# A graph-attention layer on one core: seven parts in stacked tables, and the edge term over 64 rows and 128 columns

## The chip, the cores and the metric

The kernel runs on one core of a Trainium2 chip. The metric is device time in microseconds of the whole launch, as the median of several runs. A profiled execution gives one trace beside it.

## What is computed

A graph layer over N = 12500 nodes of 128 features and E = 412500 edges with 64 features each; `dst` is sorted. It ends in two layer normalisations. The reference, cut to what matters:

```python
h = x @ Wn + bn;  q = x @ Wq + bq;  k = x @ Wk + bk;  v = x @ Wv + bv
eh = edge_attr_64 @ We + be
attn_in = concatenate([q[src], k[dst], eh], axis=-1)
hmid = leaky_relu(attn_in @ A1 + b1, 0.2)
scores = leaky_relu(hmid @ A2 + b2, 0.2)          # 8 heads
w = softmax(scores.mean(axis=-1), axis=0)         # over all edges
out = segment_sum(w[:, None] * v[dst], src, N)
y = layernorm(h + out) * gamma + beta
return layernorm(x + y)
```

The first layer `A1` is folded into the weights of q, k and the edge term, so that the hidden value of an edge is a sum of a q row (by `src`), a k row (by `dst`) and 64 edge features times a 64 x 128 matrix.

## The kernel before

Edges come sorted by `dst`, but sums are wanted by `src`. So the kernel has two halves that run interleaved.

*Making.* The edges stand in 403 groups of 1024, eight tiles of 128. For each group `make` builds one record per edge: 128 numbers of k plus edge term, 128 of v, and the source's place in its block. The k and v rows are picked by a one-hot matmul (`ohd` with `kvs`, bfloat16), and the edge term is added into the same PSUM tile `pkv` by a float32 matmul of `eat` with `WeS`. A `pkv` tile holds four edge tiles, so a group has two of them (two half-groups). In `eat` the features of tiles 0 to 3 of a group lie on partitions 0 to 63 and those of tiles 4 to 7 on partitions 64 to 127; `WeS` is a matrix of 128 rows and two times 128 columns whose off-diagonal quarters are zero, so that one matmul of 128 rows and 256 columns gives the edge term of one tile from each half. ScalarE copies `pkv` into a record tile `rec` (six buffers), and POOL scatters it to DRAM with one indirect DMA per tile, eight a group, into a table `rtab` in which every block of 128 nodes has its own stretch of `cap` rows. VectorE counts edges per block to find the rows (`few`, `ats`, `pos`, `idx`).

*Consumption.* The groups are divided into parts by `PARTS`; a part writes one of two tables in turn. Within a part there are stops: by a stop, so many tiles of every block are full with certainty, and these can be read back while the rest is written. The tiles of all 98 blocks between two stops are a round. A round is read in units of three blocks: one load `rt` of 3 x t tiles (t tiles per block, 4 or 5), then q rows by a one-hot matmul, the hidden layer (`ph`, `hm`), scores (`psc`), a running maximum, weights `w`, and the weighted sum of v rows into `psm`, which is added to the sum of the round before (`old`, kept in DRAM as `atab`). Scheduled steps of a unit are spread by `lags`; the order in which the two halves are written down is set in `sorted_path`: step lists of the rounds are laid between the six pieces of each group, from `begun[r]` on, at a pace that `PACE` sets. What remains after the last group follows alone, then `closing` normalises.

With `PARTS = (74, 140, 165), (225, 278, 307), (367, 403)` a part has 15, 13 and 9 tiles per block, 37 in all, in eight rounds of 5, 5, 5, 4, 4, 5, 4 and 5. A table holds 15 tiles per block (`cap`). Tiles that a part may leave short are filled with zeros in the first two parts (`fill`, `zeros`), and masked in the last round of a part (`masks`). Before the first round's stop, tables of q, k, v and h rows are made in pieces between the groups (`tables`, `later`), and ready by nine tenths of that stop.

All engines run their queues in order. SP issues nearly all plain DMAs in one queue: edge features and `kvs` rows four groups ahead of their use, loads and stores of units, zero fills. POOL issues the scatters; a scatter waits for its `rec` and `idx` and for the scatter eight before it.

The lines that the change and the prediction touch: L931 one-hot matmuls and L936 edge term; L946 and L947 the copies into `rec`; L958 the scatter; L1144 the load of a unit; L1243, L1247 hidden layer; L1258 scores; L1284 sum over heads; L1305 to L1323 maximum and weights; L1375 the weighted sum.

Of the kernel before, what the change touches and what calls it, by code (L numbers as in the profile page):

```python
# [10 lines left out]
FP = mybir.dt.float32  # L11
# [24 lines left out]
PARTS = (74, 140, 165), (225, 278, 307), (367, 403)  # L36
NP = len(PARTS)
NR = sum(map(len, PARTS))
# [11 lines left out]
class Plan:  # L50
# [4 lines left out]
    def __init__(self, n, e, nb, groups):  # L55
# [15 lines left out]
        most = max(self.tiles)  # L71
# [24 lines left out]

    def bounds(self):

        first = np.arange(self.nb + 1) * self.cap
        out = [first] * NP  # L100
        for p, g, t0, t in self.rounds:
            full = np.array([(t0 + t) * P] * self.nb + [0])
# [5 lines left out]
        return np.array(out, np.float32)  # L108

# [362 lines left out]
def sorted_path(  # L472
# [112 lines left out]
    WeS = const.tile([P, 2, D], FP)  # L585
# [26 lines left out]
    with tc.tile_pool(name="prep", bufs=1) as prep, tc.tile_pool(  # L612
# [164 lines left out]
    maskp = pool("mask", 1)  # L777
# [12 lines left out]
    masks, placed, lims = {}, {}, {}  # L790
    last_rounds = [r for r, q in enumerate(plan.rounds) if q[1] == plan.parts[q[0]][1]]
# [13 lines left out]
    def make(p):  # L805
# [118 lines left out]
        def rows(g, j):  # L924

            (eat, kvs), ohd = data[g], ohds[g]
            pk = pkvp.tile([P, 2, 2, 2 * D], FP, name="pkv")
            for i in range(2):
                for h in range(2):
                    t = h * (GT // 2) + j + i  # L930
                    nc.tensor.matmul(  # L931
                        pk[:, i, h, :], ohd[t], kvs,
                        start=(h == 0), stop=False,
                    )
            for i in range(2):
                nc.tensor.matmul(  # L936
                    pk[:, i, :, :D], eat[:, (j + i) * P : (j + i + 1) * P], WeS,
                    start=False, stop=True,
                )
            return pk  # L940

        def evacuate(g, j, pk):
# [7 lines left out]
                .rearrange("p (h t o) -> p t h o", h=2, o=1)[:, j : j + 2, :, :]  # L950
# [3 lines left out]
            for h in range(2):  # L954
                for i in range(2):
# [16 lines left out]
                    tc.add_to_no_dep_group(f"rows{p}.{at}", one_tile)  # L972
                    if p == 0 and g < plan.gate:
# [132 lines left out]
    def sums_of(bp):  # L1106
# [805 lines left out]
```

## Time and profile before

| | |
|---|---|
| median of 3 runs | 4827.88 us (4826.07 to 4830.85) |
| the profiled execution | 4829.19 us, of which the span of instructions 4827.2 us |
| mean granted TensorE clock | 0.916 |
| busy: PE, DVE, ACT, POOL | 3991.6, 4064.7, 3144.8, 3304.4 us |
| DMA moved | 1484.41 MB, mean 308 GB/s |
| first scatter begins, last ends | 59.3 us, 4283.7 us |

The page lists for each engine busy time and share, then the span in 40 slices with a digit for tenths of busy time. Rows of groups read: line, engine, operation, output and inputs with shapes, count, then busy time and mean duration of one in ns, then idle time ahead of them and what ended it. A wait row reads: who waited, for whom, microseconds in all, times, longest. Rows in order of time read: start, length, engine, line, operation, count. PE rows are matmul passes, PEld rows weight loads; matmuls are pipelined, so the start of one to the start of the next says more than the length of one.

### The profile page before, as it was taken

To read this page: it belongs to the slowest core of one execution; us is meant where nothing else is said; L and a number is where in the kernel's file an instruction comes from. 1 tells how busy PE (TensorE), PEld (TensorE's weight loads), DVE (VectorE), ACT (ScalarE), POOL (GpSimd) and SP (SyncE) were. 2 spreads that over 40 slices of the span, in tenths; PEclk is the share of its full clock that TensorE was granted. 3 is DMA by queue.
4 is the path that set the end of the run, shared out by engine and by line. 5 is a ranking of instruction groups with operands and counts; after the bars stand their busy time and mean duration, and the time that the engine had idled before them with its cause. 6 is when DMAs were issued, how large, how long until landed. Compare 5 with 4: busy or idle time off the path is not lost. (4 is left out here: it accounts for less than half of the span.)

```text
span 4827.2 us, 84360 instructions
## 1 busy us (share of the span) xinstructions
PE 3991.6 (83%) x26680; PEld 3111.2 (64%) x26680; DVE 4064.7 (84%) x8217; ACT 3144.8 (65%) x8198; POOL 3304.4 (68%) x3279
## 2 busy tenths in 40 slices
PE   3556655577788999999999999998998899998997
PEld 2334433466666777777777666666777777666777
DVE  8878886688878999999998888888999988877767
ACT  2432222366666778787787777777777777777886
POOL 3777777777777777777777777777777777741103
PEclk7877785899888999999999999999999999999999
DMA  6888887888988999999999999999999999989964
GB/s 196 282 279 288 286 298 243 294 300 298 296 299 299 358 336 334 333 348 337 323 335 324 329 331 329 332 336 325 342 332 326 333 316 334 320 294 327 318 215 176
DMA packets 599153, 1484.41 MB, mean 308 GB/s; under 512 B 100352, under 2 KB 299923, under 8 KB 596902
## 3 DMA queue, kind: packets, MB, share of 16 engines
q1 hardware_dynamic: 436350, 1049.04, 65.4%
q0 software_dynamic: 154752, 429.39, 23.3%
q8 instruction: 212, 3.47, 0.3%
q14 instruction: 247, 2.02, 0.1%
q10 hardware_dynamic: 7592, 0.48, 0.1%
HBM read 906.61 MB, written 611.06 MB: 314 GB/s over the span
## 5 line engine op out<-in xcount | busy, mean ns | idle before, releaser
L958 POOL DMA_INDIRECT rtab<-rec,idx x3224 | 3219.2, 999 | 1061.2 <-issue 777.2
L946 ACT ACTIVATE rec<-pkv 128x1024 f32<-128x1024 f32 x806 | 822.2, 1020 | 1120.4 <-DMA rtab<-rec,idx 572.8
L1346 ACT ACTIVATE ohw<-ohs,w 128x128 f32<-128x128 bf16 x3626 | 1189.1, 399 | 75.7 <-DVE ohs L1332 27.2
L1375 PE MATMUL psm<-rt,ohw 128*128 128x128 f32 x7252 | 1023.1, 285 | 1.1 <-ACT ohw L1346 1.0
L1375 PEld LDWEIGHTS psm<-rt,ohw 128*128 128x128 f32 x7252 | 943.9, 197 | 76.1 <-ACT hm L1243 7.7
L936 PE MATMUL pkv<-WeS,eat 128*128 128x256 f32 x3224 | 946.4, 421 | 0.0
L1247 DVE TENSOR_TENSOR hm<-ph,hm 128x512 f32<-128x512 f32 (+1 forms) x949 | 627.4, 661 | 300.9 <-ACT hm L1243 299.0
L931 PE MATMUL pkv<-kvs,ohd 128*128 128x256 bf16 x3224 | 539.1, 295 | 373.6 <-ACT rec L946 370.2
L931 PEld LDWEIGHTS <-ohd 128*128 128x128 bf16 x3224 | 320.9, 105 | 645.9 <-issue 531.8
L936 PEld LDWEIGHTS pkv<-WeS,eat 128*128 128x128 f32 x3224 | 620.2, 214 | 75.0
L1224 PE MATMUL ph<-ident,rt 128*128 128x128 f32 x3626 | 587.2, 284 | 64.5 <-DVE hm L1247 63.6
L1210 DVE TENSOR_SCALAR ohT<-rowB,iotaP,power 128x512 bf16<-128x512 uint8 (+2 forms) x1274 | 598.9, 492 | 34.8 <-DMA rowB<-row 34.6
L1243 ACT ACTIVATE hm<-ph 128x512 f32<-128x512 f32 (+1 forms) x949 | 537.5, 566 | 84.1 <-PE ph L1233 29.2
L1224 PEld LDWEIGHTS ph<-ident,rt 128*128 128x128 f32 x3626 | 418.3, 146 | 269.7 <-issue 145.5
L1233 PE MATMUL ph<-ohT,qs 128*128 128x512 bf16 (+2 forms) x2548 | 559.7, 323 | 16.1 <-DVE ohT L1210 11.3
L872 DVE TENSOR_SCALAR ohd<-dstb,node 128x1152 bf16<-128x1152 uint8 x404 | 565.0, 1399 | 4.5 <-PE pkv L931 4.5
L900 DVE TENSOR_TENSOR ats<-pc,oh 128x792 f32<-128x792 f32 x403 | 392.2, 973 | 61.7 <-PE pc L880 56.6
L1332 DVE TENSOR_TENSOR ohs<-iotaE,sl 128x512 bf16<-128x512 bf16 (+1 forms) x949 | 404.6, 426 | 5.0 <-ACT ohw L1346 4.8
L862 DVE TENSOR_REDUCE few<-oh 128x99 bf16<-128x792 bf16 x403 | 395.1, 980 | 13.9
L911 DVE TENSOR_REDUCE pos<-ats 128x8 f32<-128x792 f32 x403 | 390.7, 970 | 2.5
L1258 PE MATMUL psc<-hm,A2s 128*32 128x512 f32 (+1 forms) x1898 | 345.9, 607 | 31.9 <-DVE hm L1247 23.7
L1284 PEld LDWEIGHTS psm<-headsum,z 96*128 96x128 f32 (+2 forms) x2112 | 259.7, 193 | 32.8 <-issue 8.3
(190 smaller groups left out, 3790.5 us busy)
## 6 DMA issues: line engine op xcount, KB each, us to landing
rt<-rtab SPq DMA_DIRECT2D x160, 1950.0 KB
rt<-rtab SPq DMA_DIRECT2D x96, 1560.0 KB
eat<-in_ea SPq DMA_DIRECT2D x201, 512.0 KB
rtab<-rec,idx POOLq DMA_INDIRECT x3224
dstb<-dtab SPq DMA_DIRECT2D x201, 256.0 KB
qs<-qtab SPq DMA_DIRECT2D x256, 192.0 KB
atab<-old SPq DMA_DIRECT2D x256, 192.0 KB
old<-atab SPq DMA_DIRECT2D x224, 192.0 KB
```

The source lines that it names most:

```text
L872: nc.vector.tensor_scalar(to, row[:, cols], node, None, op0=ALU.is_equal)
L931: nc.tensor.matmul(pk[:, i, h, :], ohd[t], kvs, start=(h == 0), stop=False,)
L936: nc.tensor.matmul(pk[:, i, :, :D], eat[:, (j + i) * P : (j + i + 1) * P], WeS, start=False, stop=True,)
L946: nc.scalar.activation(rec[:, :, :, : 2 * D], pk, AF.Copy)
L958: one_tile = nc.gpsimd.indirect_dma_start(out=rtab[p % TABS][:, :], out_offset=bass.IndirectOffsetOnAxis(ap=idxs[g][:, t : t + 1], axis=0) ...
L1210: nc.vector.tensor_scalar(st["oh"][k][:, (a - t0) * P : (b - t0) * P], st["rowB"][:, a * P : b * P], iotaP, power[:, bs[u] : bs[u] + 1], o ...
L1224: nc.tensor.matmul(ph[:, j * P : (j + 1) * P], st["rt"][:, t0 + j, :D], ident, is_transpose=True, start=(j == 0), stop=False,)
L1233: nc.tensor.matmul(ph[:, cols], st["qs"][:, j0 // t, s, :], oh[:, cols], start=False, stop=(s == 1 and j1 == t0 + n),)
L1243: nc.scalar.activation(hm, state[i]["ph", k][:, : n * P], AF.Copy, scale=SLOPE)
L1247: nc.vector.tensor_tensor(hm, ph[:, : n * P], hm, op=ALU.max)
L1346: nc.scalar.activation(ohw[:, j, :], ohs[:, :, j], AF.Copy, scale=st["w"][:, t0 + j : t0 + j + 1])
L1375: nc.tensor.matmul(st["psS"][:, (1 + u) * P : (2 + u) * P], ohw[:, j, :], st["rt"][:, t0 + j, D : 2 * D], start=(k == 0), stop=(k == t - 1),)
```

## The change

It does five things. The parts become seven, ending at groups 96, 192, 243, 283, 323, 363 and 403, with stops at 60 and 156 inside the first two. That makes 9, 9, 5, 4, 4, 4 and 4 tiles per block, 39 in all, in nine rounds of 4, 5, 4, 5, 5, 4, 4, 4 and 4. The two tables shrink from 15 to 9 tiles per block, and parts may share a table at different heights: `TABLE` says which table, `ABOVE` from which tile on; parts whose tiles don't meet are told apart, so that neither waits for the other. The load of a part's last round waits for the last eight scatters of that part. The edge term is cut in two: each half of the rows of `eat` and `WeS` (64 partitions) gives its own tile by a matmul of 64 rows and 128 columns; `pkv` and `rec` are laid out half first, so that the two halves write different halves of the `pkv` tile. A second buffer for `mask`.

```diff
-PARTS = (74, 140, 165), (225, 278, 307), (367, 403)
+PARTS = (60, 96), (156, 192), (243,), (283,), (323,), (363,), (403,)
 NP = len(PARTS)
+TABLE = (0, 1, 0, 0, 1, 1, 0)
+ABOVE = (0, 0, 0, 5, 0, 4, 0)
...
-        most = max(self.tiles)
+        most = max(t + above for t, above in zip(self.tiles, ABOVE))
...
+        while any(abs(self.gate - g) < 6 for _, g, *_ in self.rounds):
+            self.gate -= 1
...
+    def apart(self, p, q):
+        a, b = ABOVE[p], ABOVE[q]
+        return p != q and TABLE[p] == TABLE[q] and (
+            a >= b + self.tiles[q] or b >= a + self.tiles[p]
+        )
...
-    WeS = const.tile([P, 2, D], FP)
+    WeS = const.tile([P, D], FP)
...
-        nc.vector.memset(WeS, 0.0)
-        for h in range(2):
-            half = slice(h * DE, (h + 1) * DE)
-            nc.vector.tensor_copy(WeS[half, h, :], We_[half, :])
+        nc.vector.tensor_copy(WeS, We_)
...
-    maskp = pool("mask", 1)
+    maskp = pool("mask", 2)
...
+            for h in range(2):
+                for i in range(2):
+                    nc.tensor.matmul(
+                        pk[:, h, i, :], ohd[h * (GT // 2) + j + i], kvs,
+                        start=(i == 0), stop=False,
+                    )
             for i in range(2):
                 for h in range(2):
-                    t = h * (GT // 2) + j + i
+                    half = slice(h * DE, (h + 1) * DE)
                     nc.tensor.matmul(
-                        pk[:, i, h, :], ohd[t], kvs,
-                        start=(h == 0), stop=False,
+                        pk[:, h, i, :D], eat[half, (j + i) * P : (j + i + 1) * P], WeS[half, :],
+                        start=False, stop=(i == 1),
                     )
-            for i in range(2):
-                nc.tensor.matmul(
-                    pk[:, i, :, :D], eat[:, (j + i) * P : (j + i + 1) * P], WeS,
-                    start=False, stop=True,
-                )
...
-                        out=rtab[p % TABS][:, :],
+                        out=rtab[TABLE[p]][:, :],
...
-                        in_=rec[:, i, h, :], in_offset=None,
+                        in_=rec[:, h, i, :], in_offset=None,
...
+                    for q in range(NP):
+                        for k in range(len(PARTS[q]) if plan.apart(p, q) else 0):
+                            for name in "rows", "loads":
+                                tc.declare_no_dep(
+                                    one_tile, group=f"{name}{q}.{k}", reason="other tiles"
+                                )
...
-            o = lags(p, nk)
+            o = lags(p, max(nk, 3))
...
+            t0 += ABOVE[p]
...
-                in_=rtab[p % TABS][bs[0] * cap : (bs[0] + m) * cap, :]
+                in_=rtab[TABLE[p]][bs[0] * cap : (bs[0] + m) * cap, :]
...
+            if r == of_part[-1]:
+                for one in tail_of[p][-GT:]:
+                    tc.add_manual_dep(
+                        rows_in, one.name, mybir.DependencyInfo(
+                            mybir.DependencyClass.Sync, mybir.DependencyReason.DATA
+                        ), reason="records of the part",
+                    )
```

TensorE, one half-group in the middle of the program, before. `ohd` and `kvs` are the one-hot and the k and v rows, `eat` the edge features, `few` the counts of a block; the last number is the size of the output.

```order
L931 MATMUL pkv<-kvs,ohd 128x256
L936 MATMUL pkv<-WeS,eat 128x2x128 x2
L880 LDWEIGHTS rest
L880 MATMUL pc<-few,rest 128x99
L1224 MATMUL ph<-ident,rt 128x128 x3
```

And a half-group there now:

```order
L944 MATMUL pkv<-kvs,ohd 128x256
L951 MATMUL pkv<-WeS,eat 128x128 x4
L894 LDWEIGHTS rest
L894 MATMUL pc<-few,rest 128x99
L1257 MATMUL ph<-ident,rt 128x128 x4
```

Two matmuls of 256 columns have become four of 128 between the same neighbours.

SP's queue at the first load of consumption, before. `eat` and `kvs` are the loads of the making, `dstb` the ids of destinations, `rt` a unit's load from table `rtab0`, and `rtab1<-zeros` fills the second table.

```order
L818 DMA eat_6065<-in_ea 128x1024
L822 TENSOR_LOAD start_224
L827 ISA
L827 DMA kvs_6070<-kvtab_65 128x256
L1144 DMA rt_6086<-rtab0_76 128x3x1300
```

And now:

```order
L832 DMA eat_5522<-in_ea 128x1024
L836 TENSOR_LOAD start_223
L841 ISA
L841 DMA kvs_5527<-kvtab_65 128x256
L1167 DMA rt_5545<-rtab0_77 128x3x1040
L588 DMA rtab1_78<-zeros_126 128x2x780
```

The first unit's load stood behind the 40th load of edge features (one for two groups) and stands behind the 33rd; it brings four tiles per block in place of five, and zero fills of the second table still follow it.

SP's queue where the last round begins, behind the last load of edge features, before. `old` and `atab` are the running sums, `qs` the q rows, `rowB` the sources of a unit.

```order
L1144 DMA rt_53491<-rtab0_76 128x2x1040
L1159 DMA qs_53554<-qtab_64 128x768
L1144 DMA rt_53570<-rtab0_76 128x3x1300
L1198 DMA rowB_53583<-row_53540 128x1536
L1404 DMA atab6_74<-old_53368 128x384
L1356 DMA old_53620<-atab5_73 128x384
```

And now:

```order
L1167 DMA rt_57861<-rtab1_78 128x2x1040
L1192 DMA qs_57924<-qtab_64 128x768
L1167 DMA rt_57940<-rtab0_77 128x3x1040
L1231 DMA rowB_57953<-row_57910 128x1536
L1437 DMA atab7_75<-old_57627 128x384
L1389 DMA old_57990<-atab6_74 128x384
```

The last round's loads go from five tiles per block to four. Behind the last load of edge features stood 7 loads of the round before and 33 of the last; now there are 9 and 33.

More of the change, by code (lines that the diff above doesn't have):

```diff
@@ L70, in __init__ @@
         ]
-        most = max(self.tiles)
+        most = max(t + above for t, above in zip(self.tiles, ABOVE))
+        assert TABLE[:TABS] == (0, 1) and not any(ABOVE[:TABS])
+        assert all(t + a <= self.tiles[k] for t, a, k in zip(self.tiles, ABOVE, TABLE))
         self.cap = most * P
@@ L790, in sorted_path @@
     masks, placed, lims = {}, {}, {}
+    tail_of = [[] for _ in plan.parts]
     last_rounds = [r for r, q in enumerate(plan.rounds) if q[1] == plan.parts[q[0]][1]]
@@ L949, in evacuate @@
                 srcl[:, g * GT : (g + 1) * GT]
[L950 removed]
+                .rearrange("p (h t o) -> p h t o", h=2, o=1)[:, :, j : j + 2, :]
                 .to_broadcast([P, 2, 2, WR - 2 * D]),
@@ L1152, in load @@
                 tc.declare_no_dep(rows_in, group=f"rows{p}.{k}", reason="tiles that are full")
+            for q in range(NP):
+                for k in range(len(PARTS[q]) if plan.apart(p, q) else 0):
+                    tc.declare_no_dep(rows_in, group=f"rows{q}.{k}", reason="other tiles")
             tc.add_to_no_dep_group(f"loads{p}.{of_part.index(r)}", rows_in)
+            if r == of_part[-1]:
[5 more added lines that the diff above has]
+                    )
             state[i] = dict(rt=rt, hm={}, oh={}, sel={})
```

7 lines of the change are left out of this document (5 added, 2 removed).

## The prediction

> **What bounds the kernel now.** I read the page first, then POOL's scatters in order of time, then busy time by stretch, then the waits, then single TensorE rows. One edge group is 1024 edges: eight scatters, and two half-groups (one `pkv` tile and one `rec` tile each).
>
> ```profile
> span 4827.2 us, 84360 instructions
> PE 3991.6 (83%) x26680; PEld 3111.2 (64%) x26680; DVE 4064.7 (84%) x8217; ACT 3144.8 (65%) x8198; POOL 3304.4 (68%) x3279
> POOL 3777777777777777777777777777777777741103
> ```
>
> TensorE and VectorE have the larger shares, but POOL's digit is what does not move: 7 in every slice from the second to the 35th, in the stretch without consumption as in the one with it. The rows of its first and last scatters say why (start, duration, what ended the idle time).
>
> ```profile
> 59.30 1.16 POOL L958 DMA_INDIRECT rtab<-rec,idx  x1 [56.02 <-DVE oh L851]
> 60.76 0.96 POOL L958 DMA_INDIRECT rtab<-rec,idx  x1 [0.30 <-issue]
> 62.02 0.96 POOL L958 DMA_INDIRECT rtab<-rec,idx  x1 [0.30 <-issue]
> 63.29 0.96 POOL L958 DMA_INDIRECT rtab<-rec,idx  x1 [0.30 <-issue]
> ...
> 4281.48 0.96 POOL L958 DMA_INDIRECT rtab<-rec,idx  x1 [0.30 <-issue]
> 4282.75 0.96 POOL L958 DMA_INDIRECT rtab<-rec,idx  x1 [0.30 <-issue]
> ```
>
> One scatter follows another after 1.265 us (60.76 to 63.29 is two), 0.96 of it busy and 0.30 for which nothing else is named. 3224 scatters from 59.3 on cannot end before 59.3 + 3223 x 1.265 + 1.0 = 4137.4. They end at 4283.7: 146 us are lost, and 543.5 us come behind them. The next rows are the scatters alone, cut where consumption rounds change: stretch, length, busy (count), granted clock, DMA share, GB/s.
>
> ```profile
> 59.29:864.70 805.41, 619.62 (x593) 0.73 0.83 274
> 864.70:1546.10 681.40, 520.51 (x528) 0.88 0.90 304
> 1546.10:2037.20 491.10, 375.26 (x381) 0.97 0.96 337
> 2037.20:2529.30 492.10, 376.28 (x381) 0.97 0.96 336
> 2529.30:2971.50 442.20, 337.37 (x344) 0.97 0.94 326
> 2971.50:3389.30 417.80, 314.35 (x318) 0.99 0.95 332
> 3389.30:3901.40 512.10, 391.75 (x395) 0.98 0.95 330
> 3901.40:4283.80 382.40, 284.10 (x288) 0.98 0.93 324
> ```
>
> Length less 1.265 per scatter (592, 528, 380, 380, 344, 317, 395, 288 of them) leaves 56.5, 13.5, 10.4, 11.4, 7.0, 16.8, 12.4 and 18.1 us of loss. Per group of eight the second to fourth and the seventh lose 0.20 to 0.25 us: there the units have 15 tiles. The sixth and eighth lose 0.42 and 0.50: units of 12 tiles, 33 of them in 39.6 groups. The fifth has 12-tile units too, but 33 in 43 groups, and loses 0.16. So the scatters pace the making, and what little is lost comes from records that are late. Who makes them late, in the eighth stretch:
>
> ```profile
> POOL rtab L958 <- ACT rec L947: 8.2, 12, 2.5
> ACT w L1323 <- DVE ref L1314: 41.5, 21, 3.2
> ACT rec L946 <- PE pkv L936: 28.7, 11, 4.5
> ACT rec L946 <- DMA rtab<-rec,idx: 8.8, 10, 3.1
> ```
>
> ScalarE waits for the matmuls of `pkv` (28.7 us) more than for scatters to free `rec` (8.8): TensorE runs level with POOL there, a little behind. Behind the making the weights (one ScalarE exponential and one accumulator read, two rows a unit) show the last units:
>
> ```profile
> 4283.70:4365.50 81.80, 2.76 (x14) 0.92 0.87 292
> 4365.50:4688.30 322.80, 13.15 (x66) 0.98 0.82 284
> 4688.30:4827.20 138.90, 0.03 (x1) 0.93 0.51 189
> ```
>
> Seven 12-tile units are left of round 6, then 33 of 15 tiles at 322.8 / 32 = 10.08 us each, then 139 us of normalising, which the change does not touch. The whole core in the early stretch and in the last round (PE, weight loads, DVE, ACT, POOL busy, clock, DMA):
>
> ```profile
> 300.00:700.00 400.00, 237.48 (x876) 164.44 (x876) 326.02 (x538) 119.72 (x181) 308.36 (x298) 0.73 0.88 288
> 4370.00:4680.00 310.00, 290.56 (x2289) 230.45 (x2287) 236.57 (x601) 268.92 (x788) 25.47 (x12) 0.99 0.83 290
> ```
>
> In the last round PE (94%) and ACT (87%) are the bound; 290.56 us over 310 / 10.08 = 30.8 units are 9.4 us of PE for a 15-tile unit, and by tiles 7.6 for one of 12 (an estimate).
>
> **The edge term.** Two matmuls of 128 rows by 256 columns become four of 64 rows by 128 columns; the trace runs each float32 matmul as two passes.
>
> ```profile
> 2510.12 0.60 PE L931 MATMUL pkv<-kvs,ohd 128*128 128x256 bf16 x4
> 2510.56 1.03 PE L936 MATMUL pkv<-WeS,eat 128*128 128x256 f32 x4
> 2511.42 0.21 PE L880 MATMUL pc<-few,rest 128*128 128x99 bf16 x1
> ```
>
> A stretch 4 us earlier:
>
> ```profile
> 2506.74 0.38 PE L1305 MATMUL psm<-ident,mx 128*128 128x128 f32 x2
> 2506.96 1.06 PE L1375 MATMUL psm<-rt,ohw 128*128 128x128 f32 x8
> 2507.94 1.32 PE L1258 MATMUL psc<-hm,A2s 128*32 128x512 f32 x8
> 2509.19 0.33 PE L1224 MATMUL ph<-ident,rt 128*128 128x128 f32 x1
> ```
>
> And weight loads of another unit:
>
> ```profile
> 1581.10 1.06 PEld L1284 LDWEIGHTS psm<-headsum,z 96*128 96x128 f32 x8
> 1582.18 0.33 PEld L931 LDWEIGHTS <-ohd 128*128 128x128 bf16 x4
> ```
>
> Before: from 2510.56 to 2511.42, 0.86 us for four passes of 256 columns, 0.215 each. A pass of 128 columns takes 0.11 (L1305: two from 2506.74 to 2506.96). The eight passes of L1375 should then be over at 2507.84; the next matmul, which uses another partition of the array (32 columns), starts 0.10 later. L1284's row holds four passes over 96 rows and four over 64; eight of 0.11 are 0.88, and 1582.18 - 1581.10 is 1.08, so about 0.18 to 0.20 goes to entering and leaving the 64-row form. Whether passes in different parts of the array run side by side is shown for columns: L1258's eight passes, six of 512 columns and two of 384, would take 6 x 0.43 + 2 x 0.32 = 3.2 us in turn by the 0.215 above, and take 1.25 with the switches.
>
> No row shows two halves of 64 rows, so I bound them. Side by side: 4 x 0.11 + 0.18 = 0.62, a saving of 0.24 us per half-group. In turn: 8 x 0.11 + 0.18 = 1.06, a loss of 0.20. I take the saving, since L1258 is the nearest row; its tiles are columns and these are rows, which keeps the other end in the range.
>
> [...]
>
> ```profile
> L1284 PEld LDWEIGHTS psm<-headsum,z 96*128 96x128 f32 x1108 | 145.3, 192 | 4.7 <-ACT z L1272 4.6
> L1284 PEld LDWEIGHTS psm<-headsum,z 128*128 128x128 f32 x960 | 121.9, 194 | 26.3 <-ACT ohw L1346 7.0 <-issue 7.0 <-ACT rec L946 4.2
> L1284 PEld LDWEIGHTS psm<-headsum,z 64*128 64x128 f32 x44 | 5.5, 187 | 1.8 <-issue 1.4 <-DVE ohT L1210 0.3
> ```
>
> 187, 192 and 194 ns for 64, 96 and 128 rows. [...]
>
> **The parts.** Tiles per block go from 37 to 39 and rounds from 8 to 9, so 297 units instead of 264 (99 of 15 tiles and 198 of 12, where there were 165 and 99). Consumption may start at group 60 and runs through the other rounds without a pause: by `PACE` (t tiles of 98 blocks plus 2.4 per unit, over 12) a round of 4 takes 39.3 groups and one of 5 takes 47.4. So 12-tile rounds cover 60-99, 156-195, 290-329, 329-369 and 369-403, 191 groups; 15-tile rounds the other 152. At each kind's own loss (0.46, the mean of 0.42 and 0.50; 0.20 to 0.24) that is 191 x 0.46 + 152 x 0.22 = 121 us, against 90 in the same place before: the extra units alone make it worse.
>
> Now the relief. Two half-groups give PE 0.48 us per group back. The fifth stretch differs from the sixth by nearly that: 33 x 7.6 us of units in 43 groups instead of 39.6 is 0.50 us per group less PE work, and the loss there is 0.16. VectorE and ScalarE are not relieved (the 41.5 us row above is theirs), so I take 0.20 for 12-tile rounds: 191 x 0.20 + 152 x 0.22 = 72 us. Bounds 0 and 121.
>
> **The early stretch.** Node tables and edge preparation are squeezed from 66.5 groups into 54, the zeroing of the second table's tails, which ran to group 157, ends at 88. What it could cost: VectorE at 326 / 400 = 82%, all of it grown by 66.5 / 54, would reach 101%; DMA 0.88 so grown 1.08, 8% of 54 groups at 805.41 / 74 us, 47 us. But the scatters and loads of the making do not grow. Loss 57 to 104, taken as 65.
>
> **The tail.** The loads of 42 units stand behind the last edge load, nine of round 7 and 33 of round 8, all of 12 tiles; before, 7 of 12 and 33 of 15. A 12-tile unit: by tiles 10.08 x 12/15 = 8.07; the seven before took 61.9 of the 81.8 us (20 passed before the first weights of the next round), 8.84 each. I take 8.4: nine units and a shorter gap 92, 32 x 8.4 = 269, then 139: 500 us (478 to 522).
>
> **Hidden or nothing.** Stacked tables: a part waits only for readers of the tiles it overwrites, whose loads stand 37 groups or more earlier (part 2 from group 192 on over part 0, whose last loads stand near 155). The added wait holds the loads of a part's last round, and behind it on SP's queue the edge and `kvs` loads; these are issued four groups ahead, 4 x 10.3 us, which covers it. SP also issues five DMAs for each of 33 more units, at no denser rate than in the sixth stretch. Four more masks and the zero fill, which shrinks, lie in VectorE's and DMA's gaps; were these full, the price would show in the 0.20.
>
> **Sum.** 4137.4 + 65 + 72 = 4274 for the last scatter, + 500 + 2.0 outside the span (4829.19 - 4827.2) = 4776. The profiled execution is 1.3 us above the median 4827.88, so 4775, 1.1% less. A change under 0.2% (10 us) is taken as none.
>
> **Rivals.**
> - No relief: late records come from VectorE's and ScalarE's turns, and PE only waits more. For it: 41.5 us of `w` waiting for `ref`. Against: the fifth stretch. 4137 + 65 + 121 + 500 + 2 = 4826, no change.
> - Halves in turn, the slower side: PE pays 0.40 us per group more at L951, in 343 groups 137 us. PE stands level with POOL, so part passes through; with half, 4826 + 69 = 4895, with all 4963. Since the extra units already use up the tail's gain, it decides as soon as 12 us get through. [...]
> - Early squeeze at its upper price: 4776 + 39 = 4815.
> - Full relief and the lower tail: 4137 + 65 + 20 + 485 + 2 = 4709.
>
> **Chances.** Forecast 0.58 (4735 to 4812, by the terms' bounds), full relief 0.07, no relief 0.17 (4812 to 4840), in turn 0.13 (4840 to 4965), early squeeze 0.05 (to 4850). The range 4730 to 4840 leaves out most of in turn and of full relief, under 0.2. Faster: 0.58 + 0.07 + a quarter of no relief and half the squeeze, 0.72; same 0.11; slower 0.17.
>
> **What would show it.** In the changed profile the two halves' passes at L951 start within some tens of ns of each other, and a half-group's edge term ends after about 0.6 us; over 1 us means in turn. The scatter period stays 1.265, group 60 starts near 59.3 + 480 x 1.265 + 65 = 731, the last scatter ends near 4274, the last round's weights come 8.4 us apart. A loss in 12-tile rounds that stays at 0.46 per group says no relief; POOL waits at 192, 283 or 363 would say that the stacked tables do collide.

## The result and the profile after

The changed kernel takes 4884.74 us (4880.29 to 4887.58, 4 runs) beside 4826.98 us (4824.23 to 4830.85) of the kernel before: a ratio of 1.0118, 95% interval 1.0101 to 1.0136. It is 1.2% slower; the forecast was 4775 us, 1.1% faster, range 4730 to 4840. In eleven of the runs below the kernel before itself took 5769 to 5834 us (last section), so each of them is read only against the runs of before made with it.

The page of the changed kernel: busy times, and POOL's digits.

```profile
PE 4090.2 (84%) x30406; PEld 3020.3 (62%) x30731; DVE 4144.1 (85%) x8393; ACT 3217.2 (66%) x8558; POOL 3305.7 (68%) x3280
POOL 3777777777777777777777777777777777760113
```

POOL still shows 7 from the second slice to the 35th; in the 36th it shows 6 where it showed 4. The scatters alone, cut at groups 60, 99, 156, 195, 243, 290, 329 and 369, where the rounds change (stretch, length, busy and count, granted clock, DMA share, GB/s):

```profile
58.58:730.90 672.32, 512.90 (x481) 0.68 0.92 300
730.90:1157.00 426.10, 305.66 (x312) 0.91 0.96 335
1157.00:1745.40 588.40, 449.47 (x456) 0.93 0.90 311
1745.40:2157.70 412.30, 307.87 (x313) 0.96 0.93 324
2157.70:2655.60 497.90, 380.86 (x384) 0.97 0.96 338
2655.60:3144.20 488.60, 371.85 (x376) 0.97 0.96 336
3144.20:3570.00 425.80, 308.01 (x312) 0.97 0.93 322
3570.00:4012.00 442.00, 315.57 (x321) 0.95 0.92 318
4012.00:4384.70 372.70, 267.91 (x272) 0.96 0.93 316
```

Length less 1.265 us per scatter (480, 312, 456, 312, 384, 376, 312, 320 and 272 of them) leaves 65.1, 31.4, 11.6, 17.6, 12.1, 13.0, 31.1, 37.2 and 28.6 us of loss. The second, fourth, seventh, eighth and ninth stretches are rounds of 12-tile units: 145.9 us in 191 groups, 0.76 each, where 0.20 was forecast. The rounds of 15 tiles lose 36.7 us in 152 groups, 0.24, as forecast.

Part of this loss is no waiting. A usual scatter is busy 0.96 us, and some last longer: busy time less 0.96 per scatter is 38.1 us in the rounds of 12 tiles (1505.0 - 1528 x 0.96), 0.20 per group, and 34.8 us in those of 15, 0.23. What lengthens them no run shows. So the rounds of 15 tiles hardly wait at all (1.9 us), and those of 12 wait 107.8 us, 0.56 per group. The same sum on the prediction's rows of before gives, for its fifth stretch, 337.37 - 344 x 0.96 = 7.1, which is the whole of its loss of 7.0; for its sixth 10.0 of 16.8, and for its eighth 7.6 of 18.1.

The stretches behind the last scatter, by the rows of the weights:

```profile
4384.70:4473.10 88.40, 3.57 (x18) 0.98 0.82 287
4473.10:4747.20 274.10, 12.97 (x66) 1.00 0.82 291
4747.20:4885.90 138.70, 0.12 (x2) 0.93 0.51 189
```

501.2 us, where 543.5 stood before and 500 was forecast; 274.10 / 32 is 8.57 us a unit. So the tail gave its 42 us, and the last scatter ends 101 us later than before.

What the rounds differ in is seen in the waits (engine and line, what was waited for: us in all, times, longest). First the round of 15 tiles from 1157 to 1745 us:

```profile
ACT rec L961 <- DMA rtab<-rec,idx: 64.2, 38, 4.1
ACT rec L961 <- PE pkv L951: 44.9, 25, 4.8
ACT w L1356 <- DVE ref L1347: 12.7, 11, 2.1
```

ScalarE waits mostly for scatters to give a `rec` buffer back: the records are ahead. Then the last three rounds of 12 tiles, 3144 to 4384 us:

```profile
ACT w L1356 <- DVE ref L1347: 153.9, 76, 4.2
DVE hm L1280 <- ACT hm L1276: 95.5, 101, 3.4
ACT rec L961 <- PE pkv L951: 86.0, 52, 4.3
POOL rtab L973 <- ACT rec L962: 44.3, 41, 4.9
DVE sl L1206 <- DMA rt<-rtab: 42.9, 28, 4.5
PE psm L1338 <- DVE mx L1332: 37.7, 35, 3.1
```

Here POOL waits for ScalarE's record, ScalarE for TensorE and VectorE, VectorE for ScalarE and for loads, TensorE for VectorE. No engine is full: TensorE is busy 1117.52 us of these 1240.5, VectorE 1064.44, ScalarE 882.59. The waits follow each other round. One case, the rows in order of time (idle time and what ended it in brackets):

```profile
3765.00 0.18 DVE L1206 SCALAR_TENSOR_TENSOR sl<-mask,rt 128x12 bf16<-128x12 bf16 x1 [4.50 <-DMA rt<-rtab]
3766.72 0.24 PE L894 MATMUL pc<-few,above 128*128 128x99 bf16 x1 [3.55 <-DVE few L876]
3769.12 1.11 PE L1257 MATMUL ph<-ident,rt 128*128 128x128 f32 x4 [2.15 <-DVE hm L1280]
3769.49 1.31 ACT L1379 ACTIVATE ohw<-ohs,w 128x128 f32<-128x128 bf16 x4 [3.89 <-DVE ohs L1365]
3771.22 1.04 PE L944 MATMUL pkv<-kvs,ohd 128*128 128x256 bf16 x4
3772.19 1.18 PE L951 MATMUL pkv<-WeS,eat 64*128 64x128 f32 x8
3773.42 1.02 ACT L961 ACTIVATE rec<-pkv 128x1024 f32<-128x1024 f32 x1 [1.70 <-PE pkv L951]
3774.82 0.96 POOL L973 DMA_INDIRECT rtab<-rec,idx  x1 [5.32 <-ACT slT L1221]
```

VectorE stands 4.5 us in front of the load of a unit whose own matmuls come later; the one-hots and counts of the making, which are behind it in the queue, begin only after it (L865 at 3765.09 us, L876 at 3765.69, L886 at 3766.59), so TensorE, then ScalarE, then POOL stand too. A scatter that should have come at 3769.8 comes at 3774.8, just behind its record's copy (3773.42 + 1.02, and L962); the `slT` that the row names ended in the same 0.3 us.

The stall is paid twice. TensorE had stood idle 3.55 and 2.15 us, and its granted clock, 1.00 from 3760 to 3764 us, is 0.50 from 3767 to 3772: the late record's one-hots (L944) and edge term (L951) take 1.04 and 1.18 us, where at full clock they take 0.60 and 0.71. Counted in the trace, the scatters behind group 60 waited 109.9 us in 80 waits of over 0.1 us. Of these, 35 waits with 77.8 us, among them all over 2 us, are for records in whose last 7 us the clock stood at 0.5 for more than 0.5 us; of all records 19% are such. How much of a wait comes from the clock alone no run separates.

How far the records are ahead can be counted: the end of the k-th copy of a source column (L962, the last step of a record) against the start of the first of its four scatters, as a mean over 16 records. In microseconds, by the group where the 16 begin:

| group | 128 | 184 | 240 | 296 | 344 | 376 |
|---|---|---|---|---|---|---|
| before | 19.8 | 6.8 | 5.5 | 1.8 | 17.4 | 2.3 |
| after | 20.0 | 2.1 | 2.7 | 1.1 | 1.2 | 1.1 |
| edge term alone (i1) | 19.7 | 7.1 | 16.3 | 12.3 | 10.8 | 1.0 |
| parts alone (i2) | 19.5 | 1.4 | 5.7 | 1.0 | 1.0 | 1.2 |
| no edge term (i3) | 19.7 | 3.0 | 9.7 | 12.3 | 1.3 | 1.7 |
| unscaled (i4) | 19.9 | 10.9 | 14.4 | 13.5 | 4.1 | 1.6 |

The lead is a store of up to 20 us, four records of four scatters. While it lasts, a late unit costs the scatters nothing. Before, it stood near 20 us up to group 150, went down through the rounds that follow, was filled again by the 15-tile round at groups 320 to 350, and was used up in two places only: groups 296 to 318 and 376 to 403. Their scatters, in the trace of before:

```profile
3158.50:3389.30 230.80, 171.40 (x174) 0.99 0.94 327
3994.20:4283.80 289.60, 213.29 (x216) 0.98 0.92 325
```

Less 1.265 for 174 and 216 scatters, 10.7 and 16.4 us: 0.49 and 0.61 us per group of eight. After, the lead is 1 to 4 us from group 60 to 99, full only in the round from 99 to 156, 2 to 6 us from 184 to 288 and near 1 us from there to the end. Why the 15-tile rounds from 195 to 290 don't fill it again was not looked into by a run of its own; with less work on ScalarE (i4) they do. In i4 no scatter waits more than 0.4 us between groups 96 and 353, through two and a half rounds of 12 tiles: the same rounds, with a lead, lose nothing to late records.

### The profile page after: what moved, and what is told of

Same layout as the page of the kernel before. It is cut to its first block, busy times and chain, and to the rows that moved or that the text cites. A ratio compares the mean times of both kernels' runs of the same rounds, so it can differ in the third digit from the quotient of the medians.

```text
span 4885.9 us, 92915 instructions
## 1 busy us (share of the span) xinstructions
PE 4090.2 (84%) x30406; PEld 3020.3 (62%) x30731; DVE 4144.1 (85%) x8393; ACT 3217.2 (66%) x8558; POOL 3305.7 (68%) x3280
## 5 line engine op out<-in xcount | busy, mean ns | idle before, releaser
L973 POOL DMA_INDIRECT rtab<-rec,idx x3224 | 3220.1, 999 | 1161.2 <-issue 769.3
L1379 ACT ACTIVATE ohw<-ohs,w 128x128 f32<-128x128 bf16 x3822 | 1250.5, 399 | 105.5 <-DVE ohs L1365 63.6
L1408 PE MATMUL psm<-rt,ohw 128*128 128x128 f32 x7644 | 1111.9, 290 | 2.7 <-ACT ohw L1379 2.2
L1280 DVE TENSOR_TENSOR hm<-ph,hm 128x512 f32<-128x512 f32 x981 | 658.0, 671 | 272.3 <-ACT hm L1276 268.7
L944 PE MATMUL pkv<-kvs,ohd 128*128 128x256 bf16 x3224 | 538.0, 294 | 157.8 <-ACT rec L961 141.1
L1243 DVE TENSOR_SCALAR ohT<-rowB,iotaP,power 128x512 bf16<-128x512 uint8 (+3 forms) x1176 | 602.2, 527 | 40.9 <-DMA rowB<-row 40.4
L951 PE MATMUL pkv<-WeS,eat 64*128 64x128 f32 x6448 | 633.8, 320 | 0.0
L1276 ACT ACTIVATE hm<-ph 128x512 f32<-128x512 f32 x981 | 560.8, 572 | 61.9 <-PE ph L1266 25.2
L944 PEld LDWEIGHTS <-ohd 128*128 128x128 bf16 x3224 | 319.2, 105 | 452.9 <-issue 323.6
L951 PEld LDWEIGHTS pkv<-WeS,eat 64*128 64x128 f32 x6448 | 468.5, 205 | 193.3 <-issue 189.6
L886 DVE TENSOR_SCALAR ohd<-dstb,node 128x1152 bf16<-128x1152 uint8 x404 | 565.0, 1399 | 0.0
L1266 PE MATMUL ph<-ohT,qs 128*128 128x512 bf16 (+3 forms) x2027 | 520.1, 341 | 35.6 <-DVE ohT L1243 18.8
L1365 DVE TENSOR_TENSOR ohs<-iotaE,sl 128x512 bf16<-128x512 bf16 x981 | 409.7, 418 | 0.8 <-ACT ohw L1379 0.8
L876 DVE TENSOR_REDUCE few<-oh 128x99 bf16<-128x792 bf16 x403 | 395.1, 980 | 13.9
L1356 ACT ACTIVATE w<-S,ref 128x12 f32<-128x12 f32 (+3 forms) x297 | 89.8, 302 | 396.2 <-DVE ref L1347 391.3
```

Of the source, the lines that this page charges most:

```text
L886: nc.vector.tensor_scalar(to, row[:, cols], node, None, op0=ALU.is_equal)
L944: nc.tensor.matmul(pk[:, h, i, :], ohd[h * (GT // 2) + j + i], kvs, start=(i == 0), stop=False,)
L951: nc.tensor.matmul(pk[:, h, i, :D], eat[half, (j + i) * P : (j + i + 1) * P], WeS[half, :], start=False, stop=(i == 1),)
L973: one_tile = nc.gpsimd.indirect_dma_start(out=rtab[TABLE[p]][:, :], out_offset=bass.IndirectOffsetOnAxis(ap=idxs[g][:, t : t + 1], axis=0) ...
L1243: nc.vector.tensor_scalar(st["oh"][k][:, (a - t0) * P : (b - t0) * P], st["rowB"][:, a * P : b * P], iotaP, power[:, bs[u] : bs[u] + 1], o ...
L1266: nc.tensor.matmul(ph[:, cols], st["qs"][:, j0 // t, s, :], oh[:, cols], start=False, stop=(s == 1 and j1 == t0 + n),)
```

## The experiments

Theory A: the loss comes with the parts. 12-tile rounds follow each other without a pause, the lead runs out, and then every wait between the engines' queues reaches the scatters; time given to TensorE goes into its own waits. Rival B is the forecast's relief: time given to TensorE shortens the 12-tile rounds. Rival C: the edge term in its new form is what costs.

**The edge term alone, the parts alone.** The edge term in the kernel before, all else as before (i1):

```diff
-    WeS = const.tile([P, 2, D], FP)
+    WeS = const.tile([P, D], FP)
...
-                    pk[:, i, :, :D], eat[:, (j + i) * P : (j + i + 1) * P], WeS,
+                    pk[:, h, i, :D], eat[half, (j + i) * P : (j + i + 1) * P], WeS[half, :],
```

> The kernel before with the new edge term alone, where before takes 4825 us. Theory A (the loss sits in the rounds of 12 tiles, which lose 0.8 to 0.9 us per group once the records have no lead; the edge term gives 0.13 us per half-group and little comes of it): 4800 to 4825 us, ratio 0.995 to 1.000, merged loss 70 to 90 us. Rival B, the forecast's relief: merged loss near 40, ratio 0.990. Rival C (twice the matmuls, in 64-row form, cost more than they give): ratio 1.004 to 1.012.

And the changed kernel with that undone (i2):

> The changed kernel with the edge term of before. Theory A: the whole loss is here, ratio 1.012 to 1.020 (4885 to 4925 us). Rival B: 12-tile rounds lose 1.1 to 1.2 us per group without TensorE's relief, ratio 1.024. Rival C: parts alone no slower than before, 0.995 to 1.002.

i1: 4823.06 us beside 4828.08, ratio 0.9988 (0.9979 to 0.9998). i2: 4880.74 us, ratio 1.0112 (1.0091 to 1.0132). The whole loss is in the parts; rivals B and C both fall. What in the parts costs it (33 more units, rounds of 12 tiles, their order, the waits where a part ends) no run took apart; theory A rests on where the lead is and where the scatters wait. The scatters of i1 in its fifth, sixth and last stretches (groups 235 to 278, 278 to 318, 368 to 403):

```profile
2532.70:2976.80 444.10, 339.25 (x345) 0.97 0.94 326
2976.80:3391.40 414.60, 315.91 (x321) 0.98 0.94 330
3908.10:4286.80 378.70, 276.41 (x280) 0.97 0.92 321
```

They lose 8.9, 9.8 and 24.5 us, where before lost 7.0, 16.8 and 18.1: the last scatter ends at 4286.8, 3 us later than before. TensorE's relief is real, and the table above shows where it went: into a lead of 12 to 16 us at groups 240 to 296, which the scatters, paced by POOL, cannot use, and which is gone again when the last round begins. The four 12-tile rounds of i2 that lie on 60-99, 290-329, 329-369 and 369-403:

```profile
732.90:1156.20 423.30, 310.13 (x313) 0.93 0.96 336
3144.70:3571.00 426.30, 310.05 (x313) 0.96 0.92 320
3571.00:4004.70 433.70, 315.71 (x320) 0.97 0.95 323
4004.70:4370.80 366.10, 270.10 (x272) 0.99 0.94 321
```

28.6, 31.6, 28.9 and 22.0 us in 152 groups, 0.73 each, without any relief; with it, 128.3 us in the same rounds, 0.84.

The busy times say why so little came through. i2's page:

```profile
PE 4091.6 (84%) x27209; PEld 3163.1 (65%) x27507; DVE 4141.3 (85%) x8395; ACT 3216.5 (66%) x8558; POOL 3316.9 (68%) x3280
```

TensorE is busy 4091.6 us with the old term and 4090.2 with the new one, although 806 half-groups at 0.12 us less (measured below) are 97 us. Its mean granted clock is 0.939 to 0.940 in the runs of i2 and 0.912 to 0.914 in those of the changed kernel; beside it before has 0.915 to 0.928, i1 0.889 to 0.896, and there 53 us of busy time are left of the 97 (3938.4 for 3991.6). So TensorE, given time, ran at a lower clock, and in the changed kernel that used up the gain. Whether the lower clock also makes the records later was not tested.

The same two kernels had been run twice earlier, where before took 5834 and 5771 us:

> The kernel before with the edge term alone in the new form (64 rows, 128 columns; pkv and rec laid out half first); parts, tables and pace as before. Theory A, reservoir: records finished ahead of POOL (up to 20 us of them) pay for stretches in which consumption is denser than POOL's pace; once they are used up, every group takes as long as the engines' waits for each other make it, not as long as TensorE is busy, so TensorE time given back turns into waiting: 4815 to 4827 us. Theory B, TensorE time: 0.13 us per half-group (0.73 measured in place of 0.86) counts wherever POOL waits, and the reservoir empties later: 4795 to 4810.

> The changed kernel with the old edge term (128 rows, 256 columns, zero quarters); seven parts and stacked tables stay. Theory A: TensorE time is not what binds, 4880 to 4900. Theory B: 0.26 us per group for some 160 groups with an empty reservoir, 4885 + 42 = 4927.

> The kernel before with the new edge term alone (parts, stops and tables as before). Theory A, the rounds of 12 tiles cost about 13.1 us a unit once ScalarE's records run with no lead, whatever TensorE is given back: the edge term gives little, the time is 0 to 20 us below before (ratio 0.996 to 1.000), and the scatters' loss stays near 146 us. Rival B, the forecast's relief (0.3 us less loss for 0.5 us of TensorE): merged loss falls from 90 to about 40 us, ratio 0.990. Rival C, the 64-row form itself is what costs (twice the matmul instructions): 20 to 60 us above before, ratio 1.004 to 1.012, with the loss spread over all groups.

> The changed kernel with the edge term of before (two matmuls of 128 rows by 256 columns a half-group); parts, stops and stacked tables as changed. Theory A: the whole loss is here, ratio 1.012 to 1.020 (4885 to 4925 us where before is 4827), 12-tile rounds lose 0.8 to 1.0 us per group. Rival B: without TensorE's relief the 12-tile rounds lose 0.3 us per group more than in the changed kernel, 1.1 to 1.2, ratio 1.024. Rival C: parts alone are no slower than before, ratio 0.995 to 1.002.

There the edge term alone came out at 1.0133 (1.0102 to 1.0165) and 1.0103 (1.0081 to 1.0125), the parts alone at 1.0053 (1.0037 to 1.0070) and 1.0060 (1.0039 to 1.0082). That is the opposite split, and the changed kernel itself, where before took 5769 us, stood at 1.0130 (1.0109 to 1.0152):

> The changed kernel itself once more, beside the runs of before that the parts of the change were compared with: on a chip where before takes 4827 us the ratio is 1.012 again (4885 us). On a chip where before takes 5770 to 5835 us, where the edge term alone was 1.010 to 1.013 and the parts alone 1.005 to 1.006: if the two parts add up 1.016 to 1.019; if the edge term relieves the rounds of 12 tiles 1.005 to 1.010.

The totals nearly agree (1.0130 and 1.0118), the split does not: had the study ended there, the edge term would have been blamed.

**TensorE's time and ScalarE's.** The changed kernel without the edge term's matmuls, so that its records lack the edge term (i3):

```diff
-                        start=(i == 0), stop=False,
+                        start=(i == 0), stop=(i == 1),
...
-                    nc.tensor.matmul(
-                        pk[:, h, i, :D], eat[half, (j + i) * P : (j + i + 1) * P], WeS[half, :],
```

> The changed kernel without the edge term's matmuls (left out of the result): TensorE is given 0.74 us more per half-group. Forecast's relief: 12-tile rounds fall to 0.2 us per group, 4760 us. Theory A with TensorE as one link of a chain: 0.4 to 0.7, 4800 to 4860 us. If TensorE's time counts for nothing: 4885 us.

And with one copy for four tiles of the one-hot, scaled by the first tile's weight, so that the other three weights are left out (i4; "unscaled" in the table):

```diff
-            for j in range(n):
-                nc.scalar.activation(
-                    ohw[:, j, :], ohs[:, :, j], AF.Copy, scale=st["w"][:, t0 + j : t0 + j + 1]
-                )
+            nc.scalar.activation(
+                ohw[:, :n, :], ohs.rearrange("p e t -> p t e")[:, :n, :], AF.Copy,
+                scale=st["w"][:, t0 : t0 + 1],
+            )
```

> The changed kernel with one ScalarE copy for four tiles of the one-hot in place of four scaled ones (weights left out of the sum): ScalarE is given 3 us per unit of 12 tiles. If ScalarE's turns hold the records up: 12-tile rounds at 0.2 to 0.4 us per group, 4760 to 4810 us. If ScalarE only waits for others: 4860 to 4885 us, with the tail alone shorter.

i3 takes 4857.23 us, ratio to before 1.0064 (1.0047 to 1.0082), 27 us under the changed kernel. i4 takes 4820.44 us, 0.9980 (0.9968 to 0.9992), 64 us under it. The scatters of i3 in the same four rounds:

```profile
734.20:1152.10 417.90, 307.42 (x312) 0.90 0.98 341
3139.90:3546.90 407.00, 308.70 (x313) 0.93 0.95 328
3546.90:3976.20 429.30, 316.25 (x321) 0.94 0.94 328
3976.20:4344.40 368.20, 270.71 (x272) 0.94 0.94 319
```

and of i4:

```profile
730.80:1149.20 418.40, 306.60 (x312) 0.92 0.96 341
3129.80:3533.30 403.50, 308.37 (x313) 0.97 0.95 335
3533.30:3955.70 422.40, 316.13 (x321) 0.96 0.95 331
3955.70:4322.40 366.70, 266.54 (x272) 0.96 0.93 321
```

23.2, 12.3, 24.5 and 24.1 us for i3 (0.55 per group), 23.7, 8.8, 17.6 and 22.6 for i4 (0.48). With the edge term gone TensorE has some 1.5 us per group more (two terms of 0.75 at full clock, below) and the loss falls by 0.29; the largest piece, 18.8 of 44 us, is between groups 290 and 329, where the lead of the table still holds. In the last rounds the time goes into waiting, as i3's waits from 3140 to 4344 us show; the mean granted clock of its runs is 0.871 to 0.877, where the changed kernel has 0.912 to 0.914.

```profile
ACT w L1349 <- DVE ref L1340: 160.7, 76, 4.4
PE psm L1331 <- DVE mx L1325: 83.6, 60, 3.2
```

TensorE's wait for the maxima grows from 37.7 to 83.6 us, ScalarE's wait for the reference goes from 153.9 to 160.7. ScalarE's time is worth more, but i4 too ends with a lead of 1.6 us. So i3 comes out as theory A expected (0.4 to 0.7 per group, 4800 to 4860 us), and i4's 0.48 and 4820 us lie between its two answers. Which of the waits begins the others is not settled.

These two had also been run where before took 5771 us:

> The changed kernel without the edge term's matmuls (its result then lacks them): TensorE is given about 0.74 us more per half-group, 1.5 us per group of 10.3. Forecast's relief: at 0.3 us of loss for 0.5 us of TensorE the 12-tile rounds would lose nothing but the 0.2 of the scatters themselves; last scatter near 4260, time near 4760. Theory A (what holds a unit up is the chain of waits through VectorE and ScalarE, with TensorE as one link): the 12-tile rounds go from 0.85 to 0.4 to 0.7 us per group, time 4800 to 4860. If TensorE counts for nothing: 4885.

> The changed kernel with one ScalarE copy for four tiles of the one-hot in place of a scaled copy for each (the weights are left out of the sum): ScalarE is given about 1.0 us per four tiles, 3 us per unit of 12 tiles. If ScalarE's turns hold the records up (theory A with ScalarE as the link): 12-tile rounds from 0.85 to 0.2 to 0.4 us per group, last round's unit under 8.56, time 4760 to 4810. If ScalarE only waits for others: 4860 to 4885, with the tail alone shorter.

Ratios 0.9991 (0.9977 to 1.0005) and 1.0052 (1.0037 to 1.0067). The order is turned round there: taking TensorE's instructions away gave more than taking ScalarE's. The expected times were for before at 4827 us and can't be held against these.

**The number of matmuls.** The edge term of before as four matmuls of 128 rows by 128 columns:

```diff
-                    pk[:, i, :, :D], eat[:, (j + i) * P : (j + i + 1) * P], WeS,
-                    start=False, stop=True,
+                        pk[:, i, h, :D], eat[:, (j + i) * P : (j + i + 1) * P], WeS[:, h, :],
+                        start=False, stop=(h == 1),
```

> The kernel before with its edge term as four matmuls of 128 rows by 128 columns (zero-padded weights kept), in place of two of 128 rows by 256 columns: as many matmul instructions as the changed edge term, none over 64 rows. Eight passes of 0.11 us take the 0.86 us of before. If the number of TensorE instructions is what makes the edge term alone 1.0 to 1.3% slower on such a chip: ratio 1.008 to 1.014 here too. If it is the 64-row form (entering and leaving it): 0.998 to 1.003.

4835.07 us beside 4824.65, ratio 1.0022 (1.0013 to 1.0032): 10 us for 3224 more passes of matmul. The ratio lies within the second answer's 0.998 to 1.003, but as before took 4825 us beside it, it doesn't tell what the edge term cost where before took 5771. i1, with as many passes over 64 rows, stands at 0.9988 beside its own runs of before.

**Loads earlier, a slower pace, steps spread out.** All where before took 5834 us (the first two) or 5770 (the others). The load of a 12-tile unit four steps earlier:

```diff
-            every=max(8, L), lead=turn + 8, ...
+            every=max(8, L), lead=turn + (8 if nk > 3 else 12), ...
```

> The changed kernel with the unit loads of 12-tile rounds written down four steps earlier (lead 24 in place of 20 steps; a step is 1.6 us). Theory A with late loads: VectorE's waits for rt (60 us in round 0, of which 33 for the first load, 51 in rounds 5 to 7) mostly go and with them a good part of the loss: 4835 to 4865. If the loads are not the cause, or the six buffers give no room: 4880 to 4890.

Units paced for 11 in place of 12:

```diff
-PACE = 12
+PACE = 11
```

> The changed kernel with PACE 11 in place of 12: a 12-tile round is laid over 42.8 groups instead of 39.3, a 15-tile round over 51.7 instead of 47.4, so more units are left for after the making (round 7 is about a third done by then). Theory A: the reservoir stays filled, groups from 290 on lose 0.2 to 0.3 us instead of 0.9, the last scatter ends near 4290, and the tail is 16 units of 8.6 us longer: 4290 + 640 = 4930. Theory C, boundaries: six part boundaries of 5 us and the new waits make the loss whatever the pace, so the last scatter stays near 4350 and the time is 4990.

Units 7 steps apart in place of 8, in the changed kernel and in the kernel of i1:

```diff
-            every=max(8, L), lead=turn + 8, ...
+            every=max(7, L), lead=turn + 8, ...
```

> The changed kernel with units of 12 tiles set 7 steps apart in place of 8, at the same pace of units to groups: every wait inside a unit is given 8/7 of the time, no engine has less work. If the records are late because of the waits inside a unit (ScalarE for the reference, TensorE for the maxima): 12-tile rounds from 0.77 to 0.4 to 0.6 us per group, 4815 to 4865 us. If it is the engines' time, or the order in which their turns come: 4870 to 4900 us.

> The kernel before with the new edge term and units of 12 tiles 7 steps apart. If spreading the steps helps, it helps its three rounds of 12 tiles (52 us of loss): 4795 to 4815 us, ratio 0.994 to 0.998, and it is the fastest so far. If not: 4815 to 4835 us.

Ratios to before 1.0189 (1.0155 to 1.0223), 1.0338 (1.0304 to 1.0371), 1.0173 (1.0148 to 1.0198) and 1.0140 (1.0114 to 1.0166). The changed kernel stood at 1.0130 there and the edge term alone at 1.0103 and 1.0133, though not beside these very runs: none of the four is seen to help. Whether they would where before takes 4827 us stays open, and with it whether late loads or short steps hold a 12-tile unit up.

**Two more.** The kernel before once more, meant for its profile in that condition, and more no-operations on POOL:

> The kernel before, for its profile on such a chip (before: 5770 to 5835 us there, 4827 on the first). If what makes these chips slower is the making of records alone, the last round's weights (no scatters behind them) come 10.1 us apart as on the first chip, and POOL stands still about once per group of eight scatters, by some 3 us. If it were clocks or memory, the last round would be 20% slower too, 12 us.

> The changed kernel with four no-operations of GpSimd ahead of each scatter in place of one. Theory S: on such a chip ScalarE is told late that TensorE has finished as long as GpSimd issues scatters without a break, and goes on only once GpSimd stands still (its waits there end a median 2.4 us behind the start of the last scatter); more room between scatters then lets the word through: 5300 to 5700 us instead of 5842. If the no-operations only add to the period, 3224 x 0.06 to 0.2 us: 5860 to 6100 us or no change within 20 us.

But before took 4824.65 us beside them. h1 took 4819.54, which is only a repeat. The profiled execution of h2 took 4886.45 us, 1.7 from the changed kernel's median; the other of its two took 18625.93 us, which nothing here explains. So three more no-operations ahead of a scatter cost nothing there (one execution); the 0.06 to 0.2 us of the expectation were the author's guess, and no run shows them. Theory S was not put to the test.

## Why the prediction was wrong, by its own steps

- *What bounds the kernel: the scatters pace the making, and what is lost comes from late records.* The pace is right, the loss only in part: 0.2 us per group, in every round, is scatters that last longer than 0.96, and no record is late in them. Period 1.265, first scatter 58.6, and 58.6 + 3223 x 1.265 + 1.0 + 65.1 + 182.6 = 4384.4 against the last scatter's end at 4384.7.
- *The edge term side by side, 0.62 us for 0.86.* Right in kind, half the size. The changed rows, and the rows of i2 with the old term, both at full clock and with nothing waited for:

```profile
3759.21 0.60 PE L944 MATMUL pkv<-kvs,ohd 128*128 128x256 bf16 x4
3759.74 0.71 PE L951 MATMUL pkv<-WeS,eat 64*128 64x128 f32 x8
3760.39 0.22 PE L894 MATMUL pc<-few,rest 128*128 128x99 bf16 x1
```

```profile
2506.20 0.60 PE L948 MATMUL pkv<-kvs,ohd 128*128 128x256 bf16 x4
2506.63 1.03 PE L953 MATMUL pkv<-WeS,eat 128*128 128x256 f32 x4
2507.50 0.21 PE L897 MATMUL pc<-few,rest 128*128 128x99 bf16 x1
```

  From start to start the eight passes take 3760.39 - 3759.74 = 0.65 us, the four of before 2507.50 - 2506.63 = 0.87. But the new ones also begin 0.53 us behind the start of the one-hots where the old begin 0.43 behind: 0.10 more in front of the first 64-row pass. So 0.75 stands for 0.87, and the gain is 0.12, not 0.24, per half-group. The rival of halves in turn (1.06) did not happen, though its 4895 lies near the result: a right time for a wrong reason.
- *The relief.* This is the step that failed: "The fifth stretch differs from the sixth by nearly that: 33 x 7.6 us of units in 43 groups instead of 39.6 is 0.50 us per group less PE work, and the loss there is 0.16". The 0.16 is the longer scatters alone: with a lead of 5 to 7 us no scatter of the fifth stretch waited, so the stretch holds no price for TensorE's time. In the sixth the lead ran out in its middle. Besides, fewer units per group are less work for VectorE and ScalarE too, not for TensorE alone. Taking 0.20 for the 12-tile rounds thus meant that no scatter would wait there; they waited 107.8 us. And the 0.48 us per group to be given back were 0.25, which the lower granted clock took back in the changed kernel. i1 and i2 show that this relief brought nothing in the 12-tile rounds.
- *The price of 12-tile rounds without relief, 0.46.* Also wrong, for the same reason: a mean of groups with a lead and groups without. Where the lead was gone the trace of before already showed 0.49 and 0.61. The new order lays four 12-tile rounds where it is gone, and they lose 0.73 (i2) and 0.84 (after). The two steps together are 145.9 - 191 x 0.20 = 108 us of the 111 by which the last scatter missed 4274. The rival "no relief", 4826, had a mechanism that fits (TensorE only waits more), with this price too low.
- *15-tile rounds, 0.22.* 0.24 measured, nearly all of it longer scatters.
- *Early stretch, 65 us; group 60 at 731.* 65.1 us, 730.9, and the rival of a dearer squeeze falls. The 65 was chosen between 57 and 104, not worked out, so the close hit is in part luck: longer scatters are 51 us of it (512.90 - 481 x 0.96), as they were before (50 of 56.5), and the squeeze added mostly waiting.
- *Tail, 500 us, 8.4 a unit.* 501.2 us, 8.57. Right.
- *Stacked tables cost nothing.* Only partly answered. The sign named was POOL waiting at 192, 283 or 363. In the trace POOL waits 8.5 us at groups 190 to 192, 6.0 at 322 and 323 and 3.9 at 362 and 363, 1.2 at 95, and not at all at 243 and 283: 20 of the 108 us lie at ends of parts. All are at the first of a record's four scatters, so waits for late records, and i4, with the same tables and a lead, has none at 192, so they show no collision of the tables; a price of their own was not measured. The row at 3765 above is a late load in the middle of a round.

## What to carry to other kernels

Where one engine paces the work and the others run ahead of it, measure the lead, not the waits: a stretch that loses little may be living on a store that an earlier stretch filled, and its loss is no price for the same work placed where the store is empty. Price such a stretch only on the part of it where the lead is gone. Take off first what the pacing engine's own instructions cost: here 0.2 us per group were longer scatters and no waits. Time given to TensorE, which waits for others, showed here as lead (16.3 us at group 240 in i1 for 5.5 before), as waits (83.6 us for the maxima in i3 for 37.7 in the changed kernel) and as a lower granted clock (0.94 in i2, 0.91 in the changed kernel); such time is worth something only if the pacing engine can use it.

## What the runs showed of the hardware

The matmuls of L951 over the two halves of the rows ran side by side: in the changed kernel's trace the passes of the two halves start in pairs 7 ns apart (2504.684 and 2504.691 us, then 2504.897 and 2504.904, and from there a pair every 0.11 us), and eight passes of 64 rows by 128 columns take 0.65 us from start to start (3759.74 to 3760.39), where eight of 128 columns in turn would be 0.88, an estimate by the 0.11 of L1305 in the prediction. The first of them starts 0.53 us behind the start of the one-hots, i2's 128-row term 0.43.

TensorE's granted clock fell where its work did: to 0.50 behind the stall at 3765 us, and in the means of the profiled executions from 0.940 with the old edge term (i2) to 0.912 with the new and 0.877 with none (i3), all in seven parts. Of the 97 us that the new term gives nothing is left in the busy time; of some 600 that its absence gives (an estimate, 806 x 0.75) 449 are (4090.2 - 3641.7, the page of i3).

One and the same program took 20% longer in some runs: on one chip before took 5768.6 us (beside g1) and, some minutes later, 4824.7 (beside h1). The changed kernel's profile in the former (g1: POOL's digits, and the last round behind the last scatter):

```profile
POOL 4776665566665555566555556655555555653103
5425.20:5701.00 275.80, 12.71 (x64) 0.99 0.82 290
```

The last round takes 275.80 us beside 274.10, so without scatters the core was hardly slower; where POOL scatters, behind group 60, it waits for over 1 us 376 times, once in about 13 us (median 2.9 us), 1077 us in all. The pages give 2121.0 us of idle time ahead of all scatters there and 1161.2 in the other profile of the same program. No run here shows the cause; the three other executions of that kernel took as long as the profiled one (5840 to 5850 us).
